# A two-layer graph network on one core: own rows of nodes loaded by groups of 512, four groups ahead, and runs of edges three steps ahead

## The chip, the cores and the metric

The kernel runs on one core of a Trainium2 chip. The metric is the time of one execution on the device, in microseconds (us). Every time below comes from the timed runs of the kernel before or from one profiled execution of it.

The engines by the profile's names: PE is the matmul engine and PEld its weight loads, DVE the vector engine, ACT the scalar engine, POOL the GpSimd engine, SP the engine that only issues transfers. A name with a "q" behind it (SPq, ACTq) is that engine's instruction queue, where it issues transfers or waits. One detail of the profile matters throughout: a transfer is issued by SP, ACT or POOL, and runs later on the core's 16 DMA engines.

## The reference

There are N = 50000 nodes with 128 features each and E = 850000 edges, sorted by their target; 50000 of the edges are loops from a node to itself. Each edge has one of 16 relations. A layer sums the source rows of a node's incoming edges by relation, multiplies each relation's sum by that relation's matrix, and adds the node's own row times a loop matrix. The 16 relation matrices are mixed from 8 basis matrices.

```python
def _rgcn_layer(h, src, dst, rel, basis, w_comp, loop_w, bias):
    W = jnp.einsum('rb,bio->rio', w_comp, basis)
    seg = dst.astype(jnp.int32) * N_REL + rel.astype(jnp.int32)
    agg = jax.ops.segment_sum(h[src], seg, num_segments=N_ENT * N_REL)
    agg = agg.reshape(N_ENT, N_REL, -1)
    msg = jnp.einsum('nri,rio->no', agg, W)
    out = msg + h @ loop_w + bias
    return jax.nn.relu(out)

h = _rgcn_layer(x, src, dst, rel, basis1, w_comp1, loop_w1, bias1)
h = _rgcn_layer(h, src, dst, rel, basis2, w_comp2, loop_w2, bias2)
x = _layernorm(x + h)
```

## The kernel before

**Tiles of edges.** The 800000 edges that are not loops are cut into 6250 tiles of 128 per layer. Ten tiles make one step `c` of the main loop (line 1086), 625 steps per layer; half a step is five tiles. For each tile the 128 source rows lie in SBUF, one row per partition. One matmul (line 1123) multiplies them with a 0/1 matrix `hot` that DVE has built and that carries the edges' weights. ACT copies the products away (line 1137), PE multiplies them with the basis matrices (line 806, a batch of four steps at a time) and a further matmul (line 850) adds them to the sums of their group of nodes.

**How rows are gathered.** Most tiles are gathered by POOL: one indirect DMA per tile (line 184, called from `fetch`, line 1067) reads 128 rows of 512 bytes. There is a ring of 30 such tiles, and POOL may issue a tile's gather as soon as the tile 30 places ahead of it has been used by PE. Every 9th or 10th half step has its last tile fetched in another way (`row_by_row`, line 1008): SP (every 9th) or ACT (every 10th) issues 128 transfers of one row each (line 1033) and reads the rows' addresses 32 at a time (line 1026). Those tiles are not in the ring; each of the two engines has three places for them. The rows of such a tile are issued during the 9 or 10 half steps that end four half steps before its use (`LEAD`).

**Groups of nodes.** The 50000 nodes are 98 groups of 512. A group's own rows, the loop edges' sources, pass through `from_itself` (line 713), a generator that the main loop calls twice per step (line 986, in `beside`). It takes the group's rows from a tile `h_own` of 128 partitions, turns them with 16 transposes (line 736), multiplies them with the basis matrices (line 756), weighs them on DVE (line 763) and sums them (line 771). A group occupies 32 partitions of `h_own`, with 16 rows of 512 bytes, 8 KB, in each. So `h_own` holds four groups. At every fourth group (`at == 0`, line 717) SP loads four groups with one transfer of 1 MB (line 720), and the transposes follow some half steps later. There is only one buffer (`bufs=1`), so the load waits for the last transposes of the four groups before. Group 97 is short: the last load of a layer brings two groups in 53 partitions, 424 KB.

**Finishing a group.** When a group's sums are complete, DVE adds the loop part. Layer 1 stores the result as H1 (line 877) and layer 2 stores the normalized rows as the output (line 883), both with transfers on SP. In layer 2 SP also loads the group's rows of x (line 849). Layer 2 gathers from H1 what layer 1 gathered from x.

**Runs of edges.** In the first half of layer 1, a generator `later_rows` (line 910) prepares the lists of sources for later steps. The main loop takes one piece of it per step (line 1090). It alternates `runs` (line 319), which loads a stretch of edges (lines 292 and 337) and packs it, with `rows_of` (line 452), which loads packed edges (line 459) and turns them into lists. After issuing its loads, each of the two yields once, and so DVE first touches the data one step later (lines 343 and 466).

**Order.** The order of instructions on each engine is the order of the program (line 926, a schedule by hand). SP's queue therefore holds, one after another: rows for its own tiles, loads of x, stores of results, loads of `h_own`, and loads for the runs. An instruction that waits holds up all that are behind it.

```python
                if at == 0:
                    end = min((g + T) * GN, N)
                    owns[0] = sb.tile([P, A * J, D], F32, name="h_own", bufs=1)
                    nc.sync.dma_start(
                        owns[0][: (end - g * GN) // (A * J)],
                        of[g * GN : end, :].rearrange("(p s) d -> p s d", s=A * J),
                    )
                h = owns[0][at : at + rows_in]
```

Of the kernel before, what the change touches and what calls it, by code (L numbers as in the profile page):

```python
# [39 lines left out]
F32 = mybir.dt.float32  # L40
# [10 lines left out]
P = 128  # L51
# [25 lines left out]
J = 4  # L77
A = 4
NEAR = 128
BATCH = 4  # L80
LAG = BATCH + 2
FIRST = 16
EPS = 1e-5

# [6 lines left out]
def tile_rgcn_resnorm(  # L91
# [15 lines left out]
    nc = tc.nc  # L107
    N, D = x.shape
# [5 lines left out]
    GN, NGR = J * P, -(-N // (J * P))  # L114
    T = P // NR // 2

    ROWS = list(range(0, 2 * C, P)) if 2 * C <= P else [0, FIRST, *range(P - 8, 2 * C, P)]
    NP = NG * P * LIVE
# [168 lines left out]
    def read(j, to, first, step, length, by=nc.sync):  # L287

        whole = max(0, min(P, (E - length - first) // step + 1))
        at = j * E + first  # L290
        if whole:
            by.dma_start(
                to[:whole], bass.AP(tensor=edges.tensor, offset=edges.offset + at, ap=[[step, whole], [1, length]])
            )
        for row in range(whole, P):
            left = min(E - first - row * step, length)
            if left > 0:
                by.dma_start(
                    to[row : row + 1, :left],
                    bass.AP(tensor=edges.tensor, offset=edges.offset + at + row * step, ap=[[left, 1], [1, left]]),  # L300
                )
# [17 lines left out]
    def runs(g, pool, asked):  # L319
# [15 lines left out]
        if ends:  # L335
            nc.vector.memset(s_i, 0)
        read(0, s_i, r0 * RUN, RUN, RUN)
        if g:
            yield
        halves = word.bitcast(U16).rearrange("p (e h) -> p e h", h=2)  # L340
        quarters = word.bitcast(U8).rearrange("p (e q) -> p e q", q=4)
# [110 lines left out]
    def rows_of(j, pool):  # L452
# [5 lines left out]
        for h in range(2):  # L458
# [1 line left out]
                parts[h][:read],  # L460
                FULL[h * NP + r0 * LIVE : h * NP + (r0 + read) * LIVE].rearrange("(p e) w -> p e w", e=LIVE),
            )
        if j:
            yield
        srcf = pool.tile([P, LIVE], F32, name="both")
        nc.vector.tensor_tensor(srcf[:m], parts[0][:m, :, 0], parts[1][:m, :, 0], op=OP.add)
# [140 lines left out]
    def chunked():  # L607
        with (
# [10 lines left out]
            def nodes(g):  # L619
                return min(GN, N - g * GN) // J  # L620

            def first(g):
                return max(0, -(-(g * GN - NEAR) // (N // C)) - 1)
# [43 lines left out]
            def ask_loops(g, n):  # L667

                end, few = min(N, (g + T) * GN), min(T, NGR - g)
                if n == 0:  # L670
                    while stored[0] < min(NG, -(-(end + NEAR) * E // (N * RUN * P))):
                        next(coming)
                    loaded[0] = end
                asked[0] = hp.tile([2 * T, GN], F32, name="lrel", bufs=1)
                nc.sync.dma_start(
                    asked[0][: 2 * few],
                    bass.AP(
                        tensor=LREL.tensor,
                        offset=LREL.offset + g * GN,
                        ap=[[GN, few], [NL, 2], [1, GN]],  # L680
                    ),
                )

            def loop_weights(g, n):

                few = min(T, NGR - g)
                of_nodes = asked[0]
                yield
                which_rel = ps_o.tile([P, BANK], F32, name="po")[:, : few * J]
                for j in range(J):  # L690
                    nc.tensor.matmul(
                        which_rel.rearrange("p (t j) -> p j t", j=J)[:, j],
                        of_nodes[: 2 * few].rearrange("q (p j) -> q j p", j=J)[:, j],
                        twos[: 2 * few, :few],
                        start=True,
                        stop=True,
                    )
                both = hp.tile([P, T * J, NR], U8, name="both_kinds", bufs=1)
                nc.vector.tensor_tensor(
                    both[:, : few * J],  # L700
                    col[:, None, 1 : NR + 1].to_broadcast([P, few * J, NR]),
                    which_rel[:, :, None].to_broadcast([P, few * J, NR]),
                    op=OP.is_equal,
                )
                yield
                lw = hp.tile([P, T * J, NB], F32, name="lw")
                for k in range(0, few * J, K):
                    m = min(K, few * J - k)
                    terms = summed_over(both[:, k : k + m], m)
                    nc.vector.tensor_reduce(lw[:, k : k + m], terms, AX.X, OP.add)  # L710
                yield lw.rearrange("p (t j) b -> p j t b", t=T)

            def from_itself(g, of, n):

                m = nodes(g)
                at, rows_in = g % T * (P // T), m // A
                if at == 0:
                    end = min((g + T) * GN, N)
                    owns[0] = sb.tile([P, A * J, D], F32, name="h_own", bufs=1)
                    nc.sync.dma_start(  # L720
                        owns[0][: (end - g * GN) // (A * J)],
                        of[g * GN : end, :].rearrange("(p s) d -> p s d", s=A * J),
                    )
                h = owns[0][at : at + rows_in]
                if g % T == 0:
                    for some in loop_weights(g, n):
                        if some is not None:
                            lws[:] = [some]
                        yield
                else:  # L730
                    yield
                lw = lws[0]
                po = ps_o.tile([P, BANK], F32, name="po")
                few = P // A
                for i in range(A * J):
                    nc.tensor.transpose(  # L736
                        po[:, i * few : i * few + rows_in], h[:, i, :], ident[at : at + rows_in, at : at + rows_in]
                    )
                    if i % (2 * A) == 2 * A - 1:
                        yield  # L740
                hT = sb.tile([P, J, P], F32, name="hT", bufs=2)
                nc.scalar.copy(  # L742
                    hT.rearrange("d j (p a) -> d a j p", a=A)[:, :, :, :rows_in],
                    po.rearrange("d (a j p) -> d a j p", a=A, j=J)[:, :, :, :rows_in],
                )
                hTs[g] = hT
                yield
                ls = sb.tile([P, J, D], F32, name="ls")
                lss[g] = ls
                few = BANK // D  # L750
                if g == 0:
                    nc.vector.tensor_copy(by[:, NB, :], BIAS[n])
                for j in range(J):
                    for b in range(0, NB, few):
                        hb = ps_o.tile([P, BANK], F32, name="po")
                        nc.tensor.matmul(  # L756
                            hb[:m],
                            hT[:, j, :m],
                            BASIS[n][:, b : b + few, :].rearrange("p b d -> p (b d)"),
                            start=True,  # L760
                            stop=True,
                        )
                        nc.vector.tensor_tensor(  # L763
                            by[:m, b : b + few, :],
                            hb[:m].rearrange("p (b d) -> p b d", d=D),
                            lw[:m, j, g % T, b : b + few, None].to_broadcast([m, few, D]),
                            op=OP.mult,
                        )
                        if b + few < NB:
                            yield  # L770
                    nc.vector.tensor_reduce(ls[:m, j, :], by[:m].rearrange("p b d -> p d b"), AX.X, OP.add)  # L771
                    yield
# [154 lines left out]
            for n, of in enumerate((x, H1)):  # L927

                weighed_for, kinds_of, own_of = {}, [None], [None]
                aTs, st, hots, masks, sums, lss, xws, hTs, lws, ending, owns = {}, {}, {}, {}, {}, {}, {}, {}, [], [], [None]  # L930

                by = hp.tile([P, NB + 1, D], F32, name="by", bufs=1)
                def hot_of(c):
# [18 lines left out]
                def added_in(c):  # L952

                    if c < ALONE:
                        return [c - LAG] if c >= LAG else []
                    at = ALONE - LAG + 2 * (c - ALONE)
                    return list(range(at, min(at + 2, C)))

                def own_of_all():

                    for g in range(NGR):
                        while now[0] < min(first(g) + LAG - 5, C - LAG - 2):
                            yield
                        if g == n == 0:
                            ask_loops(g, n)
                        elif g % T == T // 2 and g + T // 2 < NGR:
                            ask_loops(g + T // 2, n)
                        yield from from_itself(g, of, n)
                        made[0] = g + 1
                    if n == 0:  # L970
                        ask_loops(0, 1)

# [113 lines left out]
                for c in range(C):  # L1086
# [27 lines left out]
                    for k in range(0, K, PER):  # L1114
# [3 lines left out]
                        for i in range(PER):  # L1118
# [13 lines left out]
                            if i == m - 1:  # L1132
                                at = c * K + k + RING * PER
# [218 lines left out]
```

## Time and profile before

| what | value |
|---|---|
| time, median of 3 runs (lowest to highest) | 15212.37 us (15206.86 to 15213.72) |
| the profiled execution's own time | 15211.72 us |
| its span, first to last instruction | 15209.8 us |
| mean granted clock of TensorE | 0.806 |
| PE busy, share of the span | 11727.4 us, 77% |
| POOL busy | 11359.3 us, 75% |
| DVE busy | 10281.8 us, 68% |
| ACT busy | 2146.8 us, 14% |

Layer 1 takes the first half of the span and layer 2 the second; layer 2's first gather starts at about 7641 us. No engine is busy all the time by this table. The idle time that the profile puts down to "issue" is time in which an engine waited for nothing that the profile shows; on POOL it lies between two gathers, and it belongs to the gather. Issuing transfers isn't counted as busy, so SP has no row here, though it works most of the time. A wait that the profile names is put down to whatever ended last. PE idle for "DMA h_own" says that PE stood at the first transpose of a group until the load of its rows had landed.

### The profile page before, as it was taken

To read this page: it belongs to the slowest core of one execution; us is meant where nothing else is said; L and a number is where in the kernel's file an instruction comes from. 1 tells how busy PE (TensorE), PEld (TensorE's weight loads), DVE (VectorE), ACT (ScalarE), POOL (GpSimd) and SP (SyncE) were. 2 spreads that over 40 slices of the span, in tenths; PEclk is the share of its full clock that TensorE was granted. 3 is DMA by queue.
4 is the path that set the end of the run, shared out by engine and by line. 5 is a ranking of instruction groups with operands and counts; after the bars stand their busy time and mean duration, and the time that the engine had idled before them with its cause. 6 is when DMAs were issued, how large, how long until landed. Compare 5 with 4: busy or idle time off the path is not lost. (4 is left out here: it accounts for less than half of the span.)

```text
span 15209.8 us, 256696 instructions
## 1 busy us (share of the span) xinstructions
PE 11727.4 (77%) x43954; PEld 7319.2 (48%) x43954; DVE 10281.8 (68%) x11737; ACT 2146.8 (14%) x4309; POOL 11359.3 (75%) x12013
## 2 busy tenths in 40 slices
PE   6777777877777777777777888778777777777777
PEld 4444444444444444444444455445444444444444
DVE  8777777777666666666666666666666666666666
ACT  1111111111111111111111111111111111111111
POOL 6777777777777777777777777777777777777776
PEclk7888788888888888877778877887778887888787
DMA  3333333323322222222222223222222222222322
GB/s 82 74 74 74 70 75 74 70 69 72 69 62 62 62 64 62 62 62 64 57 62 66 66 66 68 66 66 66 66 67 65 66 65 67 66 66 65 68 64 58
DMA packets 584528, 1014.06 MB, mean 67 GB/s; under 512 B 265816, under 2 KB 335448, under 8 KB 576615
## 3 DMA queue, kind: packets, MB, share of 16 engines
q0 software_dynamic: 385232, 792.77, 23.3%
q1 hardware_dynamic: 131568, 186.72, 4.6%
q10 hardware_dynamic: 66064, 18.03, 1.1%
q14 instruction: 1309, 10.72, 0.2%
q8 instruction: 355, 5.82, 0.2%
HBM read 924.87 MB, written 71.59 MB: 66 GB/s over the span
## 5 line engine op out<-in xcount | busy, mean ns | idle before, releaser
L184 POOL DMA_INDIRECT g<-in_x_dram,at x5990 | 5678.2, 948 | 1891.0 <-issue 1696.8
L184 POOL DMA_INDIRECT g<-H,at x5990 | 5655.7, 944 | 1902.6 <-issue 1725.2
L1123 PEld LDWEIGHTS pa<-hot,g 128*128 128x128 f32 x25000 | 4255.5, 226 | 4267.6 <-issue 1661.8
L1123 PE MATMUL pa<-hot,g 128*128 128x96 f32 x25000 | 4795.0, 320 | 1882.3 <-DMA g<-H,at 889.9
L850 PE MATMUL pn<-slots,own 120*128 120x512 f32 x4128 | 2811.4, 809 | 669.1 <-DVE own L829 340.2
L763 DVE TENSOR_TENSOR by<-po,lw 128x512 f32<-128x512 f32 x1568 | 1074.0, 685 | 3230.7 <-PE po L756 3228.0
L1137 ACT COPY aT<-pa 128x480 f32<-128x480 f32 x2500 | 1392.0, 557 | 8104.4 <-PE pa L1123 4327.8
L806 PE MATMUL po<-aT,basis 128*128 128x480 f32 x4960 | 2359.6, 635 | 105.8 <-ACT aT L1137 105.5
L756 PE MATMUL po<-basis,hT 128*128 128x512 f32 x3136 | 1993.2, 722 | 398.7 <-ACT hT L742 335.7
L663 DVE TENSOR_REDUCE fixed<-terms 128x80 f32<-128x1280 f32 x1250 | 1864.0, 1491 | 30.4
L634 DVE TENSOR_TENSOR terms<-kinds,fixed 128x1280 f32<-128x1280 uint8 x1250 | 1848.7, 1479 | 12.2
L771 DVE TENSOR_REDUCE ls<-by 128x128 f32<-128x1152 f32 (+1 forms) x784 | 1659.2, 2116 | 33.6 <-DVE by L763 0.4
L806 PEld LDWEIGHTS po<-aT,basis 128*128 128x128 f32 x4960 | 1052.2, 219 | 1215.3 <-issue 1098.3
L850 PEld LDWEIGHTS pn<-slots,own 120*128 120x128 f32 x4128 | 914.7, 250 | 1321.0 <-issue 604.9
L939 DVE TENSOR_TENSOR hot<-fixed,own 128x960 f32<-128x960 f32 x1250 | 1438.7, 1151 | 35.0 <-PE pa L1123 7.8
L789 DVE TENSOR_TENSOR slots<-po,which 120x1024 f32<-120x1024 f32 (+1 forms) x630 | 759.8, 1206 | 264.2 <-PE po L815 238.8
L756 PEld LDWEIGHTS po<-basis,hT 128*128 128x128 f32 x3136 | 567.1, 226 | 437.5 <-ACT hT L742 363.1
L736 PE MATMUL po<-ident,h_own 32*128 32x32 f32 x3136 | 335.1, 256 | 311.5 <-DMA h_own<-H 169.8
L1060 ACT CAST at<-src 128x20 int32<-128x20 uint16 x626 | 129.5, 207 | 2414.7 <-issue 2397.3
L736 PEld LDWEIGHTS po<-ident,h_own 32*128 32x128 f32 x3136 | 288.5, 173 | 363.2 <-issue 230.9
L829 DVE TENSOR_SCALAR own<-col,node 120x256 f32<-120x256 f32 (+1 forms) x1250 | 428.5, 343 | 7.5 <-PE pn L850 7.5
L810 ACT COPY by_slot<-po 128x480 f32<-128x480 f32 x310 | 173.0, 558 | 1609.6 <-PE po L806 1404.5
(143 smaller groups left out, 3522.5 us busy)
## 6 DMA issues: line engine op xcount, KB each, us to landing
g<-in_x_dram SPq DMA_DIRECT2D x17536, 0.5 KB
g<-H SPq DMA_DIRECT2D x17536, 0.5 KB
g<-in_x_dram ACTq DMA_DIRECT2D x15744, 0.5 KB
g<-H ACTq DMA_DIRECT2D x15744, 0.5 KB
g<-in_x_dram,at POOLq DMA_INDIRECT x5990
g<-H,at POOLq DMA_INDIRECT x5990
H<-ls SPq DMA_DIRECT2D x97, 256.0 KB
xw<-in_x_dram SPq DMA_DIRECT2D x97, 256.0 KB
```

Source lines behind the costliest of these rows:

```text
L184: return nc.gpsimd.indirect_dma_start(out=to, out_offset=None, in_=of, in_offset=bass.IndirectOffsetOnAxis(ap=idx, axis=0))
L634: nc.vector.tensor_tensor(terms, kinds[:, :, None, :].to_broadcast([P, k, NB, NR]), table[:, None, :, :].to_broadcast([P, k, NB, NR]), op= ...
L663: nc.vector.tensor_reduce(to[:, : ks(i)], terms, AX.X, OP.add)
L756: nc.tensor.matmul(hb[:m], hT[:, j, :m], BASIS[n][:, b : b + few, :].rearrange("p b d -> p (b d)"), start=True, stop=True,)
L763: nc.vector.tensor_tensor(by[:m, b : b + few, :], hb[:m].rearrange("p (b d) -> p b d", d=D), lw[:m, j, g % T, b : b + few, None].to_broadc ...
L771: nc.vector.tensor_reduce(ls[:m, j, :], by[:m].rearrange("p b d -> p d b"), AX.X, OP.add)
L789: nc.vector.tensor_tensor(to[:k], of[:k, :, None, :].to_broadcast([k, pair, J, D]), which[:k, c : c + pair, :, None].to_broadcast([k, pair ...
L806: nc.tensor.matmul(ps[:, : BATCH * S], BASIS[n][:, b, :], aT[:, b, :], start=b == 0, stop=b == NB - 1)
L850: nc.tensor.matmul(sums[g], own, of[:k].rearrange("s j d -> s (j d)"), start=c == first(g), stop=c == final(g),)
L939: nc.vector.tensor_tensor(hot[:, : ks(c)], pm[:, : ks(c), :, None].to_broadcast([P, ks(c), NB, WN]), own[:, : ks(c), None, :].to_broadcast ...
L1123: product = nc.tensor.matmul(pa[:, i * NB * WN : (i + 1) * NB * WN], row, hot[:, k + i].rearrange("e b w -> e (b w)"), start=True, stop=Tr ...
L1137: nc.scalar.copy(aT[:, :, place_of + k * WN : place_of + (k + m) * WN].rearrange("d b (i w) -> d i b w", w=WN), pa[:, : m * NB * WN].rearr ...
```

## The change

`h_own` becomes one tile for the whole kernel. A new function `load_own(g, groups, of)` loads `groups` groups from group `g` on into the partitions that belong to them. At the start of a layer it loads four groups at once, as before. From then on, as soon as `from_itself(g)` has run to its end, it loads group `g + 4` alone, 256 KB in 32 partitions, into the place of group `g`; the last group has 21 partitions. Apart from that, `runs` and `rows_of` yield three times instead of once between their loads and the first use of the data.

```diff
+AHEAD = 3
...
         read(0, s_i, r0 * RUN, RUN, RUN)
-        if g:
+        for _ in range(AHEAD if g else 0):
             yield
...
-        if j:
+        for _ in range(AHEAD if j else 0):
             yield
...
+            owns = sb.tile([P, A * J, D], F32, name="h_own", bufs=1)
+
+            def load_own(g, groups, of):
+
+                at, end = g % T * (P // T), min((g + groups) * GN, N)
+                nc.sync.dma_start(
+                    owns[at : at + (end - g * GN) // (A * J)],
+                    of[g * GN : end, :].rearrange("(p s) d -> p s d", s=A * J),
+                )
+
             def from_itself(g, of, n):

                 m = nodes(g)
                 at, rows_in = g % T * (P // T), m // A
-                if at == 0:
-                    end = min((g + T) * GN, N)
-                    owns[0] = sb.tile([P, A * J, D], F32, name="h_own", bufs=1)
-                    nc.sync.dma_start(
-                        owns[0][: (end - g * GN) // (A * J)],
-                        of[g * GN : end, :].rearrange("(p s) d -> p s d", s=A * J),
-                    )
-                h = owns[0][at : at + rows_in]
+                if g == 0:
+                    load_own(0, T, of)
+                h = owns[at : at + rows_in]
...
                         yield from from_itself(g, of, n)
                         made[0] = g + 1
+                        if g + T < NGR:
+                            load_own(g + T, 1, of)
```

More of the change, by code (lines that the diff above doesn't have):

```diff
@@ L929, in chunked @@
                 weighed_for, kinds_of, own_of = {}, [None], [None]
-                aTs, st, hots, masks, sums, lss, xws, hTs, lws, ending, owns = {}, {}, {}, {}, {}, {}, {}, {}, [], [], [None]
+                aTs, st, hots, masks, sums, lss, xws, hTs, lws, ending = {}, {}, {}, {}, {}, {}, {}, {}, [], []
                 by = hp.tile([P, NB + 1, D], F32, name="by", bufs=1)
```

## The prediction, made before the changed kernel ran

> **What bounds the kernel now.** I began with the costliest groups of the page. After the mean of each gather stands the idle time before it.
>
> ```profile
> L184 POOL DMA_INDIRECT g<-in_x_dram,at x5990 | 5678.2, 948 | 1891.0 <-issue 1696.8
> L184 POOL DMA_INDIRECT g<-H,at x5990 | 5655.7, 944 | 1902.6 <-issue 1725.2
> ```
>
> Busy and idle time add up to 7569 and 7558 us per layer, 15128 of the span of 15209.8. So POOL, 75% busy by name, is hardly ever free: a gather takes 0.944 us and 0.30 of issue. That is the floor, and only POOL's further waits can be won. The timeline shows PE standing still for 14 us while POOL keeps its beat, because the ring lets it run up to 30 tiles ahead:
>
> ```profile
> 13507.76 0.94 POOL L184 DMA_INDIRECT g<-H,at  x1 [0.30 <-issue]
> 13518.99 0.94 POOL L184 DMA_INDIRECT g<-H,at  x1 [0.30 <-issue]
> 13519.36 1.06 PE L736 MATMUL po<-ident,h_own 32*128 32x32 f32 x8 [13.98 <-DMA h_own<-H]
> ```
>
> A wait of PE thus costs only what reaches POOL. So I asked for POOL's waits in five windows: 3370 to 3440 us (first row), 3440 to 7490 (second), the end of layer 1 to 7660 (next three), 10950 to 15040 in layer 2 (next two), and from 15041 on (last two).
>
> ```profile
> POOL g L184 <- PE pa L1123: 7.5, 3, 4.6
> POOL g L184 <- PE pa L1123: 69.7, 170, 7.2
> POOL g L184 <- issue: 49.1, 89, 22.3
> POOL g L184 <- PE pa L1123: 18.7, 8, 10.5
> POOL g L184 <- ACT aT L1137: 8.3, 2, 6.7
> POOL g L184 <- issue: 921.7, 3019, 0.3
> POOL g L184 <- PE pa L1123: 76.9, 148, 7.5
> POOL g L184 <- PE pa L1123: 20.7, 7, 8.3
> POOL g L184 <- ACT aT L1137: 2.0, 1, 2.0
> ```
>
> From each wait I take off the ordinary 0.305 us (921.7 / 3019). That leaves 6.6, then 17.8, then 16.3 + 7.7 = 24.0, then 31.8, then 18.6 + 1.7 = 20.3: together 100.5 us. The 22.3 us is the change of layers, which waits for H1 and stays. So 100.5 us is about all that this change can touch.
>
> Who causes those waits? The tile `h_own`, asked for 7900 to 10950 us (two rows) and 10950 to 15130 (two rows):
>
> ```profile
> L720 SPq DMA_DIRECT2D h_own<-H x10: 362/363/370, 7973.7 to 10724.0; - x10
>   DMA h_own<-H: 0.2, 1
> L720 SPq DMA_DIRECT2D h_own<-H x14: 243/362/426, 11030.3 to 15041.0; - x14
>   DMA h_own<-H: 226.2, 18
> ```
>
> The same load costs PE nothing for 3000 us and then 226 us (PE and its weight loads together). The transfer hasn't changed; it is issued later, because SP has fallen behind. SP's own waits, 7900 to 10400 us and then 10420 to 15060, its rows in 13000 to 14000, and POOL's gathers in an undisturbed millisecond:
>
> ```profile
> SPq L883 <- ACT ls L605: 81.4, 20, 8.2
> SPq L883 <- ACT ls L605: 9.0, 5, 3.9
> L1033 SPq DMA_DIRECT2D g<-H x2354: 224/228/585, 12999.8 to 13999.7; - x197
> L184 POOL DMA_INDIRECT g<-H,at x801: 940/944/1068, 8000.1 to 8999.9; - x161
> ```
>
> At first SP waits 20 times for results to store: it is ahead. Later it hardly waits. Of 450 tiles SP takes 10 and ACT 9, so POOL's 431 gathers at 801 per ms last 538 us, in which SP owes 1280 rows: 2379 per ms. It issues 2354, 1% too few. So SP is a second limit just under POOL's, and `h_own` is where its lateness shows first.
>
> **The change part by part.** *The waits at the layers' ends.* The last load of each layer, 53 partitions, stops PE for long (PE's timeline, layer 1 then 2; then the chain, with a 1 MB load for comparison):
>
> ```profile
> 7517.23 1.03 PE L736 MATMUL po<-ident,h_own 32*128 32x32 f32 x8 [27.32 <-DMA h_own<-in_x_dram]
> 15073.39 1.03 PE L736 MATMUL po<-ident,h_own 32*128 32x32 f32 x8 [19.72 <-DMA h_own<-H]
> 13503.08 16.24 DMA h_own<-H
> 15040.96 32.30 DMA h_own<-H
> ```
>
> The smaller load takes twice as long. The Trainium skill (DMA: Bandwidth & Descriptors, "Why a DMA increments its semaphore by 16 and not by 1") explains it: a transfer uses the largest number of engines up to 16 that divides its partitions, so 128 use 16 and the prime 53 one, and by that rule the new loads of 32 and 21 would use 16 and 7. The rows agree.
>
> The new loads have three groups' time, over 200 us (98 groups in 7569 us, 77 us each, three of them), for a landing between 4.1 us (a quarter of 16.24) and 19.5 (32 of 53 parts of 32.30). So these waits go. Behind them PE sets the pace: POOL waits for it until the end. In layer 1 POOL gets back 24.0 us of the 27.3; in layer 2 PE's end moves by its 19.7. Sum: **43.7 us**.
>
> *The waits in the middle.* Their share of POOL's waits is 17.8 + 31.8 = 49.6 us. If SP were ahead, all of it would be won. But SP's position doesn't depend on PE's stalls except where it waits for a store, and PE cannot use SP's tile before its rows have landed. This is already seen (PE's timeline, the chain, then two rows that show how much SP has in hand before the last stall: SP starts the next tile's addresses at 15008, PE uses the finished tile at 15038):
>
> ```profile
> 14437.77 0.74 PE L1123 MATMUL pa<-hot,g 128*128 128x96 f32 x2 [8.21 <-DMA g<-H]
> 14039.12 16.53 DMA g<-H
> 15008.28 2.23 SPq L1026
> 15036.90 2.15 PE L1123 MATMUL pa<-hot,g 128*128 128x96 f32 x18
> ```
>
> Landing takes about 14 to 16 us, and some 29 us lie between. So in layer 2 PE could come to 15038 about 14 us earlier with SP as it is, and SP's 9.0 us of waits, which follow PE's stalls, may shrink too: 23 us. Against that stands what SP has more to issue. The load itself, for 128 partitions and for 53, each with the instruction behind it:
>
> ```profile
> 13503.08 0.36 SPq L720 DMA_DIRECT2D h_own<-H  x1
> 13503.54 31.61 SPq L1033 DMA_DIRECT2D g<-H  x78
> 15040.96 0.24 SPq L720 DMA_DIRECT2D h_own<-H  x1
> 15041.30 38.87 SPq L1033 DMA_DIRECT2D g<-H  x58
> ```
>
> One costs SP 0.34 to 0.46 us; 32 partitions are nearer to 53 than to 128, but I take 0.40. There will be 95 loads per layer (one of four groups, 94 of one) for 25. Where SP is late, 10420 to 15040 us, that is 45 more, 18 us, with the rows queued behind them. Net gain in layer 2: 23 - 18 = 5 us. In layer 1 SP stops waiting near 3500 us; 39 more loads are 16 us, and I set the credit equal, net 0. So of 49.6 us I count **5**, with 49.6 and -34 (18 + 16, no credit) as ends.
>
> The Trainium skill (DMA: Bandwidth & Descriptors, "Rules for kernel authors") speaks against the change: 128 partitions and 1 MiB per transfer, and one transfer rather than several to disjoint partitions. [...]
>
> The new load stands behind the last step of `from_itself(g)` and waits for that group's transposes. This wait costs SP nothing: the last transposes before the load at 15040.96 were at 14974.42, at the same distance in the program.
>
> ```profile
> 14974.42 1.06 PE L736 MATMUL po<-ident,h_own 32*128 32x32 f32 x8
> ```
>
> *The runs.* Loads stay where they are in SP's queue; only DVE comes two steps later. In the nine blocks DVE waits 46.9 us, nearly half of it once (whole trace, then 3370 to 3440 us), when SP had lost 20 us behind another transfer:
>
> ```profile
> DVE both L466 <- DMA parts<-FULL: 46.9, 9, 20.4
> DVE both L466 <- DMA parts<-FULL: 20.4, 1, 20.4
> SPq L675 <- DMA LREL<-l_rel,l_to: 20.0, 1, 20.0
> ```
>
> Two steps are 24 us (15209.8 / 1250 each), more than 20.4, so that wait goes, and POOL's **6.6 us** with it; the other waits never reached POOL. The price: each of 19 blocks ends two steps later, 38 steps in all. Counting the generator's yields, its last block ends at step 361 of 625 instead of 325, and no list is late for its step, so nothing is caught up in a burst. If SP's 20 us wait comes elsewhere instead, the 6.6 is 0.
>
> Sum against the profiled execution's 15211.7 us (1.9 more than its span): 43.7 + 5 + 6.6 = 55.3, so 15156.4. The median of the runs is 0.7 higher: **15157 us**.
>
> **The rivals.** *All of it is won.* If fewer stalls leave SP as fast as it needs to be, 100.5 us go: 15112. For it: PE waits for SP's and ACT's rows only rarely (layer 2, then layer 1). Against: 2354 rows where 2379 are owed.
>
> ```profile
> PE pa L1123 <- DMA g<-H: 41.7, 11, 8.2
> PE pa L1123 <- DMA g<-in_x_dram: 25.4, 8, 8.4
> ```
>
> *Only part of the ends is won.* If PE comes to the last steps later than now, by SP's lateness in the middle, half of 43.7 stays: 22 less, 15190. This is within 0.2%, about 30 us, which is what a measurement here can tell from no change.
>
> *Slower: SP takes over.* If SP sets PE's pace from 3500 and from 10420 us on, its 84 more loads count in full, at the upper 0.46: 39 us, and if its last tiles also hold up PE at the ends nothing is won there: 15251. The point is where rows are issued less than about 14 us before use; the 29 us before the last stall speak against.
>
> *It doesn't do what it says.* With one tile for all, the transposes of group g + 1 could be made to wait for the load of group g + 4, issued just before. Then there are four times as many waits: 3 x 49.6 = 149 us more, 15361. The trace of before cannot show this; the code names disjoint partitions.
>
> **How the numbers follow.** Forecast 0.56, all won 0.20, part of the ends 0.14, SP takes over 0.07, wait for every load 0.03. The range reaches to the first rival on one side, 15108, and over the second on the other: with nothing from middle or runs and 34 us more on SP, 43.7 - 34 = 10, so 15203; I put 15205. Faster by over 0.2% are the forecast (but for 0.06 of it at its upper end) and the first rival: 0.70. Within: 0.06 + 0.14 and a little of the last two, 0.21. Slower: 0.09.
>
> **What would show it.** `h_own` loads: 95 per layer, PE's idle time for them near zero. POOL's waits at the two ends nearly gone. In the middle POOL should still wait some 45 us, with "DMA g<-H" or "DMA g<-in_x_dram" of those rows grown from 41.7 and 25.4 us as the cause; if POOL's waits vanish there, the first rival holds. DVE should no longer wait 20 us at line 466. The prediction is wrong if PE still idles for `h_own`, or if SP's waits for stores come back in the late stretches, for then SP was never the limit.

## The result and the profile after

| | kernel before | changed kernel | predicted |
|---|---|---|---|
| median (lowest to highest), us | 15212.19 (15203.67 to 15214.83), 6 runs | 15153.64 (15151.88 to 15158.36), 6 runs | 15157 (15108 to 15205) |
| ratio to before, 95% interval | | 0.9963 (0.995 to 0.9976) | 0.9964 |
| profiled execution, us | 15211.72 | 15153.49 | 15156.4 |

The changed kernel is faster by 58.6 us, 0.4%, more than the 0.2% (about 30 us) that a measurement here can tell from no change. What POOL has to do hasn't changed, so the gain must stand in POOL's idle time. These are the two costliest rows of the page of the changed kernel (busy time and mean of one, then the idle time before them):

```profile
L185 POOL DMA_INDIRECT g<-in_x_dram,at x5990 | 5681.6, 949 | 1850.8 <-issue 1705.0
L185 POOL DMA_INDIRECT g<-H,at x5990 | 5654.8, 944 | 1883.0 <-issue 1734.1
```

Busy and idle time are 7532.4 us in layer 1 and 7537.8 in layer 2. That is 36.8 and 20.5 us less than the 7569.2 and 7558.3 of before, together 57.3 of the 58.1 us by which the span is shorter.

Where in the layers did it come from? These are POOL's waits in the changed kernel, in stretches that answer to those of the prediction: 3340 to 3440 us (first row), 3440 to 7450 (second), 7450 to 7575 (next two), 7575 to 7640 (fifth), 10950 to 15000 (sixth), and from 15000 on (last).

```profile
POOL g L185 <- PE pa L1131: 1.8, 6, 0.3
POOL g L185 <- PE pa L1131: 41.2, 121, 3.2
POOL g L185 <- ACT aT L1145: 4.2, 1, 4.2
POOL g L185 <- PE pa L1131: 2.1, 7, 0.3
POOL g L185 <- issue: 32.0, 33, 22.3
POOL g L185 <- PE pa L1131: 69.2, 143, 5.9
POOL g L185 <- PE pa L1131: 8.3, 5, 7.0
```

I take 0.305 us off each wait, as the prediction did (the fifth row is the change of layers, where the longest wait is still 22.3 us):

| place | before | left after | won | predicted |
|---|---|---|---|---|
| runs, layer 1 | 6.6 | 0 | 6.6 | 6.6 |
| middle of layer 1 | 17.8 | 41.2 - 121 x 0.305 = 4.3 | 13.5 | 0 |
| end of layer 1 | 24.0 | 4.2 - 0.3 = 3.9 | 20.1 | 24.0 |
| middle of layer 2 | 31.8 | 69.2 - 143 x 0.305 = 25.6 | 6.2 | 5 |
| end of layer 2 | 20.3 | 8.3 - 5 x 0.305 = 6.8 | 13.5 | 19.7 |
| sum | 100.5 | 40.6 | 59.9 | 55.3 |

The ends gave 10 us less than forecast, the middle 15 us more.

The tile `h_own` in the changed kernel: its loads with their issue time in ns (least, median, greatest), and the two things for which PE stood idle before its transposes.

```profile
L719 SPq DMA_DIRECT2D h_own<-in_x_dram x95: 282/327/431, 83.7 to 7334.4; - x95
L719 SPq DMA_DIRECT2D h_own<-H x95: 282/327/467, 7601.4 to 14870.6; - x95
  issue: 26.3, 154
  DVE lw L711: 0.2, 1
```

There are 95 loads per layer, and no row names a DMA: PE never waits for `h_own` again. An issue takes 0.33 us; to SP's next instruction it is 0.37 at the median, and that is what the prediction put at 0.40. What does PE wait for instead? PE's waits in the long second part of layer 2, first the changed kernel (10950 to 15000 us), then the kernel before (10950 to 15040 us):

```profile
PE pa L1131 <- DMA g<-H: 436.5, 52, 17.3
PE pa L1131 <- DMA g<-H,at: 156.4, 208, 2.4
```
```profile
PE pa L1123 <- DMA g<-H,at: 383.0, 510, 2.8
PE po L736 <- DMA h_own<-H: 149.9, 13, 19.8
```

With the 41.7 us for single rows that the prediction quotes, PE waited 574.6 us for these transfers before, and it waits 592.9 us now. Stalls for `h_own` and waits for POOL's own gathers (`g<-H,at`) have turned into waits for single rows (`g<-H`). By the view of line 1041, which issues them, all 660.4 us that PE waits for rows in the two layers are for SP's rows, and none for ACT's. That is the new wait which the prediction named. Most of it lies in the slack of the ring, and only 25.6 us reach POOL.

SP's two longest kinds of wait in the changed kernel from 10420 to 15060 us, the stretch of the prediction, are these:

```profile
SPq L889 <- ACT ls L606: 6.2, 4, 2.2
SPq L719 <- PE pa L1131: 1.6, 6, 0.4
```

SP's waits for results to store have not come back: 6.2 us where there were 9.0, all of them before 10820. The wait that the new load brings with it (line 719) is 0.4 us at most. And the runs: SP's wait of 20.0 us for `LREL` is now one of 13.4, at another place (between 2600 and 2800 us), and DVE has one wait for `parts` left, a short one.

```profile
SPq L676 <- DMA LREL<-l_rel,l_to: 13.4, 1, 13.4
```
```profile
DVE both L467 <- DMA parts<-FULL: 7.2, 1, 7.2
```

One thing must be known for what follows: the experiments ran on three chips, and on two of them SP and ACT need much longer to issue a row, so that the kernel before takes about 23640 us there.

### The profile page after: what moved, and what is told of

It is laid out like the page before. It is cut to its first block, busy times and chain, and to the rows that moved or that the text cites. A ratio compares the mean times of both kernels' runs of the same rounds, so it can differ in the third digit from the quotient of the medians.

```text
span 15151.7 us, 257086 instructions
## 1 busy us (share of the span) xinstructions
PE 11523.2 (76%) x43954; PEld 7232.1 (48%) x43954; DVE 10284.4 (68%) x11737; ACT 2147.1 (14%) x4309; POOL 11361.0 (75%) x12013
## 5 line engine op out<-in xcount | busy, mean ns | idle before, releaser
L1131 PE MATMUL pa<-hot,g 128*128 128x96 f32 x25000 | 4701.1, 318 | 2228.5 <-DMA g<-in_x_dram,at 778.8
L856 PE MATMUL pn<-slots,own 120*128 120x512 f32 x4128 | 2758.1, 795 | 725.6 <-DVE own L835 414.2
L812 PE MATMUL po<-aT,basis 128*128 128x480 f32 x4960 | 2303.4, 622 | 103.9 <-ACT aT L1145 96.0
L777 DVE TENSOR_REDUCE ls<-by 128x128 f32<-128x1152 f32 (+1 forms) x784 | 1659.6, 2117 | 33.6 <-DVE by L769 0.4
L945 DVE TENSOR_TENSOR hot<-fixed,own 128x960 f32<-128x960 f32 x1250 | 1439.3, 1152 | 41.2 <-PE pa L1131 18.5
L866 PEld LDWEIGHTS pn<-loop,hT 128*128 128x128 f32 x1568 | 248.3, 225 | 131.0 <-issue 131.0
```

Source lines behind the costliest of these rows:

```text
L812: nc.tensor.matmul(ps[:, : BATCH * S], BASIS[n][:, b, :], aT[:, b, :], start=b == 0, stop=b == NB - 1)
L856: nc.tensor.matmul(sums[g], own, of[:k].rearrange("s j d -> s (j d)"), start=c == first(g), stop=c == final(g),)
L945: nc.vector.tensor_tensor(hot[:, : ks(c)], pm[:, : ks(c), :, None].to_broadcast([P, ks(c), NB, WN]), own[:, : ks(c), None, :].to_broadcast ...
L1131: product = nc.tensor.matmul(pa[:, i * NB * WN : (i + 1) * NB * WN], row, hot[:, k + i].rearrange("e b w -> e (b w)"), start=True, stop=Tr ...
```

## The experiments

The theory: POOL's waits came from late transfers of SP, and the late `h_own` loads were the greatest of them. What is left is late rows. Its rivals: the loads cost SP more than their waits are worth, or the wait for `h_own` was a matter of the load's size, not of its lateness. Kernels of one group below ran on one chip, beside the kernel before.

**Two halves alone, the last load as before, and more lead.** Four kernels on a chip where the kernel before takes 23659.06 us (35 runs). In the first the runs keep their old distance:

```diff
-AHEAD = 3
+AHEAD = 1
```

> The changed kernel with one step instead of three between the loads of the runs and their use; own rows still come one group at a time, four groups ahead. The theory (gathers set the beat, late in each layer SP's single rows are the second limit, and the change won what h_own cost at the layers' ends plus a little in the middle): about 7 us are lost again, the wait of 20 us at line 466 that reached POOL with 6.6 us, so 15160 us, between 15153 and 15167. Rival (the runs' part gave most of what was won in the middle of layer 1): 15170 to 15180, with POOL's waits between 3440 and 7490 us near the 17.8 us of before.

The second is the kernel before with only the runs' part of the change (`AHEAD = 3`, and the loops over it in `runs` and `rows_of`).

> The kernel before with three steps instead of one between the loads of the runs and their use, and nothing else. The theory: only POOL's 6.6 us at 3400 to 3430 us go, so 15206 us, within 5 of the kernel before (15212), and PE still idles some 400 us for h_own. Rival (the runs' part carries a good share of the gain): 15190 or less.

The third loads the last two groups together in 53 partitions again, when the first of them begins:

```diff
-                if g == 0:
-                    load_own(0, T, of)
+                if g == 0 or g == NGR - 2:
+                    load_own(g, T, of)
...
-                        if g + T < NGR:
+                        if g + T < NGR - 2:
```

> The changed kernel, but the last two groups of each layer are loaded as before: together, in 53 partitions, when the first of them begins. It puts a price on the layers' ends. The theory: POOL's waits at the ends come back, 24.0 and 20.3 us where the changed kernel has 3.9 and 6.7, so 15153 + 34 = 15187 us, between 15180 and 15200. Rival (what was won at the ends would have been waited for anyway, and the gain comes from the middle): 15153 to 15165.

The fourth has SP and ACT finish their rows eight half steps before use:

```diff
-LEAD = 4
+LEAD = 8
```

> The changed kernel with LEAD 8 instead of 4: SP and ACT finish issuing the rows of their tiles eight half steps before use, not four, so SP enters each layer with about 24 us more in hand. The theory (SP falls behind by about 1% late in each layer, and PE then waits for its rows): 24 us cover some 2400 us of falling behind, POOL's waits in the middle fall from 4.3 + 25.6 us to 8 or less, and the time to about 15130 us, between 15120 and 15140; PE's waits for rows of SP's own tiles (436 and 224 us) fall by half or more. Rival (SP is not the limit, the waits left come from PE's own work or from the DMA engines alone): no change, 15148 to 15158.

Measured: own rows alone 23696.40 us, ratio 1.0015 (1.0004 to 1.0025); runs alone 23657.96, 1.0001 (0.9992 to 1.001); the old last load 23712.32, 1.0015 (1.0005 to 1.0024); more lead 23626.95, 0.9986 (0.9977 to 0.9995). The times that the expectations give don't apply: here SP's issuing sets the pace, as this group and the next show. This is one line of SP's timeline with own rows alone, then one of the changed kernel on the usual chip:

```profile
12000.10 53.61 SPq L1041 DMA_DIRECT2D g<-H  x68
```
```profile
12008.08 34.69 SPq L1041 DMA_DIRECT2D g<-H  x80
```

In these stretches a row costs SP 0.79 us here and 0.43 there. Over the millisecond from 13000 us SP issues 1504 rows here and 2360 there, 0.66 and 0.42 us each. With runs alone, PE waits:

```profile
PE pa L1124 <- DMA g<-H: 2248.3, 105, 36.2
PE pa L1124 <- DMA g<-in_x_dram: 2192.4, 110, 40.4
PE po L737 <- DMA h_own<-in_x_dram: 682.1, 24, 48.6
PE po L737 <- DMA h_own<-H: 660.7, 24, 42.0
```

And with own rows alone:

```profile
PE pa L1131 <- DMA g<-H: 3046.0, 131, 37.5
PE pa L1131 <- DMA g<-in_x_dram: 2517.6, 109, 36.8
```

This is the lesson of the case at its largest. Between the two, the new loads take 1343 us of stalls for `h_own` away, and the kernel is 38 us slower (the runs' part alone is worth nothing here). The intervals of the two ratios overlap, so the 38 us are uncertain; that nothing was won is clear. PE's waits for rows are 1123 us longer, since what paces the kernel is SP's queue, which has become longer. The wait on `h_own` was here only the place where SP's lateness showed. The kernel with more lead isn't a clean test: by its issues it also has 128 rows fewer on each of SP and ACT in each layer (17408 and 15616 for 17536 and 15744).

**What one more load costs where SP sets the pace.** On another chip of this kind (kernel before 23615.33 us, 27 runs) I repeated two of them and changed the number of loads. Each load in four:

```diff
-                nc.sync.dma_start(
-                    owns[at : at + (end - g * GN) // (A * J)],
-                    of[g * GN : end, :].rearrange("(p s) d -> p s d", s=A * J),
-                )
+                for s in range(0, A * J, A):
+                    nc.sync.dma_start(
+                        owns[at : at + (end - g * GN) // (A * J), s : s + A],
+                        of[g * GN : end, :].rearrange("(p s) d -> p s d", s=A * J)[:, s : s + A],
+                    )
```

> The changed kernel with each of its loads of own rows cut into four by features' rows (four rows of nodes of each partition at a time): the same bytes and the same times of issue, but 380 loads per layer for SP to issue instead of 95. It multiplies the suspected cost. The theory: 285 more issues per layer at 0.33 us are 94 us of SP; early in a layer SP has some 3% in hand, which takes them, but it falls behind sooner, and from about the middle on they count in full: 40 to 60 us per layer, so 15235 to 15275 us, with PE's waits for SP's rows grown by more than half. Rival (what SP issues is hidden behind POOL's gathers): 15150 to 15165.

Two groups per load:

```diff
-                        if g + T < NGR:
-                            load_own(g + T, 1, of)
+                        if g % 2 and g + T - 1 < NGR:
+                            load_own(g + T - 1, 2, of)
```

> The changed kernel with own rows loaded two groups at a time (512 KB in 64 partitions), when the second of the two groups before them has been turned: 49 loads per layer instead of 95, still two groups ahead. The theory: 46 issues of 0.33 us less are 15 us of SP per layer, of which the late part of a layer gets back 8 to 10: 15153 - 18 = 15135 us, between 15125 and 15148; PE still does not wait for h_own. Rival (smaller loads as such are what helped, being gentler to the queue): 15158 or more.

More lead, again:

> The changed kernel with LEAD 8 instead of 4, again, for a chip on which SP issues a row every 0.32 us as in the profiles of before and after. The theory (gathers set the beat; late in each layer SP falls behind by about 1%, and PE then waits for SP's rows): 24 us more in hand cover some 2400 us of falling behind, POOL's waits in the middle fall from 4.3 + 25.6 us to 8 or less, the time to about 22 us under the changed kernel's 15153, between 15120 and 15140, and PE's waits for SP's rows fall by half or more. Rival (SP is not the limit, the waits left are PE's own work): no change, 15148 to 15158.

The old last load, again:

> The changed kernel with the last two groups of each layer loaded as before, together, in 53 partitions, when the first of them begins; again, for a chip on which SP issues a row every 0.32 us. The theory: POOL's waits at the layers' ends come back, 24.0 and 20.3 us where the changed kernel has 3.9 and 6.7, so 15153 + 34 = 15187 us, between 15180 and 15200. Rival (those waits would come anyway): 15153 to 15165.

Measured: in four 23825.99 us, 1.0087 (1.0073 to 1.0101); pairs 23583.40, 0.9984 (0.9975 to 0.9993); more lead 23603.49, 0.9992 (0.9983 to 1.0001); the old last load 23651.63, 1.0015 (1.0006 to 1.0024). The two repeats agree with the first runs. The loads of the kernel in four, then of the kernel with pairs:

```profile
L720 SPq DMA_DIRECT2D h_own<-in_x_dram x380: 3/367/1479, 101.8 to 11540.1; - x190
L720 SPq DMA_DIRECT2D h_own<-H x380: 3/367/1378, 11893.1 to 23450.8; - x190
```
```profile
L719 SPq DMA_DIRECT2D h_own<-in_x_dram x48: 3/500/578, 101.3 to 11467.7; - x48
L719 SPq DMA_DIRECT2D h_own<-H x48: 3/504/762, 11827.0 to 23231.9; - x48
```

The two differ by 760 - 96 = 664 loads and by 242.6 us, 0.365 us per load. Added up from the traces, the instructions of the loads take SP 273 us in the one and 39 in the other, 235 apart. So here the issue of a load counts in full. (The two also load at different times, so this is near to a price and not exactly one.)

This price doesn't explain every run. Against the kernel before, the old last load has 138 loads more, 50 us, and is 36 slower; own rows alone has 140 more, 51 us, and was 37 slower on its chip. But pairs have 46 more, 17 us, and are 32 faster. So pairs win some 49 us by something that isn't the issue; the other two, which also load earlier than the kernel before, win some 14 by the same reckoning. Why stays open. In the old last load PE also waits for the 53 partitions:

```profile
  DMA h_own<-H: 42.7, 1
  DMA h_own<-in_x_dram: 39.7, 1
```

Own rows alone has no such waits, and both stand at 1.0015 of the kernel before. What these 82 us of waits cost on these chips is too little to be seen. The changed kernel itself wasn't run on them.

**Without the loads on SP.** These four ran on a chip of the usual kind (kernel before 15210.68 us, 10 runs). First the changed kernel again:

> The changed kernel once more. On a chip with SP at 0.32 us per row: 58 us less than the kernel before, as measured. On a chip like those of the last two calls, where SP needs about 0.7 us per row and the kernel before takes 23615 to 23659 us: the theory says that SP alone sets the pace there, so taking 1340 us of PE's waits for h_own away gains nothing and 140 more loads on SP cost 50 to 100 us by their issue: 1.001 to 1.003 of the kernel before. Rival (waits of PE for h_own cost time wherever they stand): 0.98 or less.

Measured: 15152.79 us (15149.86 to 15158.36), 0.9962 (0.9948 to 0.9976). Then the same with its loads of single groups on ACT's queue:

```diff
-                nc.sync.dma_start(
+                (nc.scalar if groups == 1 else nc.sync).dma_start(
```

> The changed kernel with the loads of single groups issued by ACT instead of SP: same number, size and place in the program. The theory (what a load costs is its place in SP's queue): on a chip with SP at 0.32 us per row some 15 us less than the changed kernel; on one with 0.7 us, where SP alone sets the pace, 94 issues per layer leave SP, 60 to 130 us less than the changed kernel. Rival (the size or number of the loads, or the DMA engines that move them, cost the time): same time as the changed kernel, within 15 us.

Measured: 15161.74 us (15157.05 to 15165.66), 0.9968 (0.9956 to 0.998), so 9 us slower than the changed kernel where 15 faster was expected. That is what the rival said, within its 15 us. PE's waits for rows with the loads on ACT, then in the repeated changed kernel:

```profile
PE pa L1131 <- DMA g<-in_x_dram: 408.5, 54, 13.9
PE pa L1131 <- DMA g<-H: 339.2, 50, 15.2
```
```profile
PE pa L1131 <- DMA g<-H: 365.3, 49, 14.8
PE pa L1131 <- DMA g<-in_x_dram: 213.9, 34, 15.0
```

PE waits 747.7 us for rows without the loads on SP, and 579.2 with them (660.4 in the first profile of the changed kernel). In all three it is SP's rows alone that PE waits for. SP's row issues between 12000 and 14000 us: the kernel before, the changed kernel, the loads on ACT.

```profile
L1033 SPq DMA_DIRECT2D g<-H x4715: 224/228/660, 11999.8 to 13999.7; - x197
```
```profile
L1041 SPq DMA_DIRECT2D g<-H x4710: 224/228/612, 11999.9 to 13999.9; - x197
```
```profile
L1041 SPq DMA_DIRECT2D g<-H x4716: 224/228/561, 11999.9 to 13998.8; - x197
```

4715, 4710 and 4716 rows: the same to 6 rows, whoever issues the loads. (They are moved to ACT here, not left out, and ACT's own rows stand behind them then.) So of the 18 us that 45 more loads were to cost, nothing is seen on the usual chip. Something else seems to set the pace of SP's rows there. The Trainium skill (DMA: Bandwidth & Descriptors, "Issuing engines are not separate DMA queues") says that SP and ACT share the same 16 DMA engines, so that issuing on several only saves the time it takes to issue. Here not even that time was won.

**Half the rows.** If lateness is the cause, then a kernel with few rows on SP should not wait for `h_own` even with the old loads. I gave SP and ACT every 20th half step each (from half step 40 on), once in the kernel before and once in the changed one:

```diff
-SPANS = (9, 10)
+SPANS = (20, 20)
...
-            for q in range(20 + span * i // len(SPANS), 2 * C - LEAD, span):
+            for q in range(40 + span * i // len(SPANS), 2 * C - LEAD, span):
```

The kernel before with it:

> The kernel before with the two helpers relieved: SP and ACT each fetch every 20th half step's last tile (the first at 40) instead of every 9th and 10th; POOL gathers the others, some 139 more per layer. With SP far ahead all through a layer, gathers alone set the pace: 2 x 6129 gathers at 1.2485 us are 15304 us, and with 153 us at the start, the change of layers and the end some 15460 to 15500 us on any chip. The theory (h_own is waited for because SP is late): PE's waits for h_own vanish between the ends of the layers, though nothing is done to the loads, and only those of the 53-partition loads at the ends are left. Rival (the load is issued too late by its place in the program): PE waits some 400 us for h_own, as in the kernel before.

The changed kernel with it:

> The changed kernel with SP and ACT relieved in the same way as in the run beside it. The theory: with SP ahead there is no late h_own to mend but at the layers' ends, so it is 5 to 35 us faster than that run, not 58, and its extra 140 loads on SP cost nothing. Rival (the waits for h_own in the middle are the load's own): 50 us or more faster than that run.

Measured: 15432.98 us, 1.0147 (1.0131 to 1.0162), and 15432.17, 1.0146 (1.013 to 1.0161). The two are the same, where a difference was expected. In the kernel before with half the rows: the `h_own` loads of layer 2 and the largest part of PE's idle time before the transposes, then the largest of POOL's waits for PE, then SP's from 10820 to 15060 us.

```profile
L720 SPq DMA_DIRECT2D h_own<-H x25: 244/362/366, 7750.6 to 15254.7; - x25
...
  issue: 26.8, 157
```
```profile
POOL g L184 <- PE pa L1123: 110.1, 361, 0.3
```
```profile
SPq L883 <- DVE ls L879: 1811.8, 55, 45.5
```

The same 25 loads per layer, the last with 53 partitions, cost PE nothing, at the ends too. SP waits 1812 us for stores: it is ahead. So the wait for `h_own` was lateness and not size.

The landings in the traces show two parts of this lateness, and the prediction's "The transfer hasn't changed; it is issued later" saw only one. Take the 1 MB loads of layer 2 in the kernel before. Those between 7974 and 9799 us were issued 12 to 23 us before PE was ready for the transposes, those from 11030 on 11 us at most. But they landed later as well. 15 of a load's 16 parts land within 6 us all along. The last part lands 5.0 us after the issue in the load at 7974, 12.7 at 9187, and 14 to 18 from 11030 on. With half the rows, a whole load of 1 MB lands in 4.8 to 7.3 us in layer 2, and PE comes 31 to 54 us after its issue. An estimate from these figures: had the loads from 11030 on landed in 5 us, each issued as late as it was, PE would have waited some 23 us for them and not 150. So what held up the landing did as much as the late issue.

The price is 139 gathers more per layer: 278 x 1.25 = 347 us on POOL, less the 100.5 of waits and some 9 at the change of layers, 237 in all; measured 222.

What makes the rows late, if not SP's own load? This is the time to land of POOL's ten indirect writes of `LREL` in layer 1, which are issued as its gathers are (least, median, greatest): in the kernel before, then in the kernel before with half the rows.

```profile
DMA to landing us min/median/max: 2.2/12.6/17.8
```
```profile
DMA to landing us min/median/max: 2.2/2.2/5.8
```

With many rows in flight, POOL's own transfers take 12.6 us instead of 2.2. So rows and gathers meet in the DMA engines. My own count of the landings in the trace points to one engine: of a gather's 16 parts, in layer 2 from 12000 to 14000 us, the 15th lands 2.54 us after issue in the kernel before, the last 13.6 us after; with half the rows 2.48 and 2.54. The Trainium skill (DMA: Bandwidth & Descriptors, "Why a DMA increments its semaphore by 16 and not by 1") has a transfer that can't be divided run on one engine, and on the queues of SP and ACT always on the lowest-numbered. Single rows would then all go through one engine. The trace agrees: the load of 53 partitions has one late landing (and one entry at its issue) where a load of 128 has sixteen, and 128 single rows have some 253 such entries, two a row. The old last load fits too: with its 53 partitions it took 32.30 us on the usual chip and 18.46 us where SP issues fewer rows (chain of waits of the second kernel with the old last load):

```profile
23488.24 18.46 DMA h_own<-H
```

The kernel before also shows that a slow transfer in flight can hold up SP. These are SP's issues of rows in the 32 us while the load of 53 partitions is in flight (15041 to 15073 us), then in the 33 us before it:

```profile
L1033 SPq DMA_DIRECT2D g<-H x44: 228/266/2807, 15041.3 to 15072.8; - x44
L1033 SPq DMA_DIRECT2D g<-H x73: 227/228/424, 15008.0 to 15040.7; - x73
```

SP issues 44 rows instead of 73, and a single issue takes up to 2.8 us. So the issue of a row is itself held up by what is ahead of it. That the rows, all on one engine, hold themselves up in this way late in a layer, and so set SP's pace, is likely by this and not shown: no experiment spread the rows over other engines.

No kernel here is faster than the changed one on the usual chip. Pairs, own rows or runs alone, the old last load and more lead weren't measured there.

## Why the prediction was right

**What bounds the kernel** held: POOL's waits were what could be won, 100.5 us of them, and 59.9 were. That a stall of PE costs only what reaches POOL is why the end of 311 us of PE's waits for `h_own` (31 of them) gave 58 us.

**The ends, 43.7 predicted, 33.6 measured.** The loads no longer stop PE, as forecast. The step "in layer 1 POOL gets back 24.0 us; in layer 2 PE's end moves by its 19.7" took all of POOL's wait to be the load's. Behind the load, PE waits for DVE in the work of the layers' last groups. PE's timeline of the changed kernel, at the end of layer 1 and of layer 2:

```profile
7563.31 3.74 PE L784 MATMUL po<-basis,aT 128*120 128x128 f32 x16 [3.19 <-DVE by L769]
15102.51 3.39 PE L784 MATMUL po<-basis,aT 128*120 128x128 f32 x16 [4.76 <-DVE by L769]
```

Just there POOL waits its last 4.2 and 7.0 us. This is what comes late next once the load is on time; I had looked only at the load. The kernel before has the same two waits, 3.19 us at 7601 and 4.76 at 15161, so its trace showed them. But the kernel before with half the rows has two such waits of PE as well, and at its ends POOL's largest wait for PE is an ordinary one (all of PE, then POOL from 15250 us on):

```profile
PE po L778 <- DVE by L763: 7.0, 2, 3.8
```
```profile
POOL g L184 <- PE pa L1123: 0.9, 3, 0.3
```

So it seems to take both, this work and a PE that comes to it late because of the rows; no run separates the two.

**The middle, 5 predicted, 19.7 measured.** Its limit was seen rightly: single rows, SP's, are late, they are what PE waits for now, and so not all of the 49.6 us is won. The forecast "POOL should still wait some 45 us" turned out as 4.3 + 25.6 = 29.9. Two steps were mis-sized. In layer 1, "39 more loads are 16 us, and I set the credit equal, net 0": 13.5 of 17.8 us were won. In layer 2, "18 us, with the rows queued behind them": SP's rows come at the same rate with the loads and without, so nothing is seen of that price. But the credit of 23 us wasn't won either. That the 5 came out near the measured 6.2 is luck: two terms were too large. Behind both stands the reading that SP is late by its own work. About half of the load's lateness was its landing, and the pace of SP's rows seems to be set in the DMA engines.

**The runs, 6.6,** came as forecast. The 20.4 us wait of DVE is 7.2, and POOL has none there. No run removed this part alone on the usual chip, so that it is worth 6.6 us rests on the profile.

**The sum.** 55.3 us against 58.6 is closer than its terms, and that is luck too: 10 us too much at the ends and 15 too little in the middle.

**The signs named.** 95 loads, no wait for `h_own`, rows as the cause of what is left (PE's waits for them rose from 41.7 and 25.4 us to 436.5 and 223.9), no 20 us wait on DVE, no return of SP's waits for stores: as forecast. Two came in part: at the ends 10.7 of POOL's 44.3 us are left ("nearly gone"), and in the middle 29.9 where some 45 were forecast.

**The rivals.** All won: no, 40.6 us are left. Only part of the ends: its reason, a PE that comes late to the last steps, holds, as far as the kernel with half the rows tells; but 10 of the 43.7 us are missing, not half, and the middle made up for them. SP takes over: not on the usual chip, but on the two others it is what happens, with 0.365 us per load where the rival had 0.46 at most. Wait for every load: no, the load of group g + 4 stops nobody.

## What to carry to other kernels

A wait named after a load may tell of the queue that issues it, or of the other transfers in flight, and not of the load: compare the same load early and late in the run, its issue and its landing, before giving it a buffer or splitting it. When a late transfer is moved ahead in a queue that has no slack, others become late. So count the gain at the engine that ends last, here POOL: PE's waits were as long after as before. And before taking the whole of a wait as won, ask what the work behind it would have waited for by itself.

## What was not expected of the hardware

- The same program takes 15211 us on some chips and 23615 to 23659 on others. On both, most rows are issued 0.32 us apart. But with own rows alone SP's timeline has 8339 pauses of 0.6 to 0.8 us between instructions, and in the changed kernel on the usual chip 2. The granted clock is also lower there, 0.70 instead of 0.81. Why is open.
- Transfers of one row, issued by SP and ACT, make POOL's own transfers land late (12.6 us at the median against 2.2) and the last part of a 1 MB load as well (14 to 18 us against 5), though the DMA engines are busy only some 30% of the time on the mean.
- What an issue on SP costs the kernel depends on what sets SP's pace: 0.365 us, all of it, where issuing does, and too little to be seen where it doesn't.
